# A Mamba-2 recurrence in chunks of 64 tokens instead of 128, two chunks side by side on the partitions

## The chip, the cores and the metric

The kernel runs on one core of a Trainium2 chip. Its engines are TensorE (PE; weight loads are listed apart as PEld), VectorE (DVE), ScalarE (ACT), GpSimd (POOL) and SyncE (SP), which issues nearly all DMAs. The metric is the device time of one launch in microseconds (us); lower is better. All arithmetic is in float32.

## The reference

The kernel computes one transformer-like layer on 8 sequences of 2048 tokens with 256 channels: a normalisation modulated by a condition, a Mamba-2 block, a gated residual, a second modulated normalisation, and 8 dense experts with a thresholded softmax gate. The change touches the recurrence of the Mamba-2 block, which the reference itself writes in chunks:

```python
CHUNK = 64                                   # NHEADS 8, HEADDIM 64, D_STATE 128
dA_cs = jnp.cumsum(dtc * A, axis=2)          # within a chunk
xt = xc * dtc[..., None]
diff = dA_cs[:, :, :, None, :] - dA_cs[:, :, None, :, :]
Lmat = jnp.where(causal, jnp.exp(diff), 0.0)
scores = jnp.einsum('bcihn,bcjhn->bcijh', Cc, Bc) * Lmat
y_diag = jnp.einsum('bcijh,bcjhp->bcihp', scores, xt)
decay_states = jnp.exp(dA_cs[:, :, -1:, :] - dA_cs)
states = jnp.einsum('bcjhn,bcjh,bcjhp->bchpn', Bc, decay_states, xt)
chunk_decay = jnp.exp(dA_cs[:, :, -1, :])
# scan over the chunks: s = chunk_decay * s + states; prev_states is s before each chunk
y_off = jnp.einsum('bcihn,bcih,bchpn->bcihp', Cc, jnp.exp(dA_cs), prev_states)
y = y_diag + y_off                           # + x * D, times silu(z), normalised, times W_out
```

The length of the chunk doesn't change the mathematical result: a longer chunk has a larger triangle of token pairs and fewer states.

## The kernel before, in words

The tokens are worked on in 32 blocks of T = 512 (4 for each of 8 sequences), each in NC = 4 chunks of P = 128 tokens. Each block passes through stages written as Python generators: `first_norm`, `project_xbc` (with `conv` and `steps_of_time`), `project_z`, `silu_xbc`, and for each chunk `spread`, `turn`, `within`, with `outputs` once for two chunks; then `output`, `gate_weights` and `experts`. A planner runs all generators on one simulated clock: a stage starts at its time in `STARTS` plus n * 70 us, each `yield` puts its next step later by so many us, `until` waits for a step of another stage, and `take` and `give` hand out the 8 PSUM banks (at most 4 for the use "m", two at once for the outputs). The order in which the steps come up is the order of the instructions on each engine; at run time each engine works through its own list in that order and waits on semaphores where data is missing. The plan's times are not enforced on the chip. So a changed `yield` changes the order alone.

The steps that the change touches:

- `steps_of_time` (L491): the step sizes dt of 8 heads for 4 chunks stand on 32 partitions a chunk. A scan (L526) forms the running sums `cs` of dt * A along the 128 tokens of a chunk, one DMA writes them to DRAM (L529), ACT forms the decays to the end of the chunk (L531), and PE turns dt, cs and the decays to token-major, `tok_major` (L535, L539).
- `spread` (L543): for each chunk a DMA spreads the sums of all heads over 128 partitions, `wide`, [128, 8 heads, 128 tokens].
- `turn` (L552): a transposing DMA brings x and B of the chunk token-major into `xtok`.
- `within` (L565): ACT forms for each head relu(cs_j - cs_i) on a 128x128 square, `w` (L575); PE forms the scores B.C (L585); ACT takes exponentials of `wide` (L586) and of `w` (L587); DVE scales x by dt (L590), masks the scores (L594) and multiplies them into `w` (L604); POOL scales x by the decays, `xdec` (L600), copies the decay of the whole chunk, `whole` (L608), and multiplies `wide` by C (L609). Then PE forms the state update B.xdec (L620), POOL decays the old state (L623), DVE adds (L634). Each state is [128 states, 512].
- `outputs` (L640): for two chunks, PE adds for each head x.w and state.wide into one PSUM bank a chunk (L652): 8 + 8 matmuls, 64 weight columns, 128 tokens each. DVE adds x * D (L664) and multiplies by silu(z) (L668); ACT squares (L675); POOL sums the squares to `sqs` (L677, L678).
- `output` (L685): 5.0 us of plan after the last outputs of a block, PE sums `sqs` over partitions (L693) and applies W_out (L706).

The other lines named in the prediction: L437 and L484 are the input projections, L366 the transposes of normalised tokens, L498, L733 and L812 small matmuls for dt, the gate and the expert biases, L741 and L772 transposes of the gate, L825 the experts' matmuls, and L782 their weighted sums on DVE.

Of the kernel before, what the change touches and what calls it, by code (L numbers as in the profile page):

```python
# [13 lines left out]
ALU = mybir.AluOpType  # L14
AX = mybir.AxisListType

P = 128
# [9 lines left out]
def kernel(  # L27
# [39 lines left out]
    NSB = L // T  # L67
    HALO = D_CONV - 1
    QD = P // NC
    assert NH <= QD and NH == 2 * MI and D_STATE == P and L % T == 0 and DI == NH * HEADDIM and DI <= 512 and CD == DI + 2 * P  # L70

    n_names = [0]
# [11 lines left out]

    ident = new(const, [P, P], "ident")
    make_identity(nc, ident)
    masks = new(const, [P, 2, P], "masks")
    ones, upper = masks[:, 0, :], masks[:, 1, :]
    nc.gpsimd.memset(ones, 1.0)
    make_upper_triangular(nc, upper, val=1.0, diag=True)  # L90
    neg_half = new(const, [P, NC], "neg_half")
    nc.gpsimd.memset(neg_half, -0.5)

# [397 lines left out]
    def steps_of_time(n):  # L491
# [31 lines left out]

        cs = new(sml, [P, P], "cs", bufs=1)
        nc.vector.tensor_scalar(u, dt, a_neg, None, ALU.mult)
        nc.vector.tensor_tensor_scan(cs, ones, u, 0.0, ALU.mult, ALU.add)  # L526
        yield 4.0
        d["cs_d"] = new(dram, [P, P], "cs_d")
        nc.sync.dma_start(out=d["cs_d"], in_=cs)  # L529

        nc.scalar.activation(e, cs, AF.Exp, bias=cs[:, P - 1 : P], scale=-1.0)  # L531
        yield 7.0
        t_ps = yield from take("m")
        for i, t in enumerate((dt, cs, e)):
# [8 lines left out]
    def spread(n, c):  # L543

        yield from until(info[n], "cs_d")
        wide = info[n]["wide", c] = new(chk, [P, NH, P], "wide", bufs=4)
        nc.sync.dma_start(
            out=wide, in_=info[n]["cs_d"][c * QD : c * QD + NH, :].partition_broadcast(P)
        )
        yield  # L550

# [13 lines left out]
    def within(n, c):  # L565


        d = info[n]
        yield from until(d, "tok", ("wide", c))
        xbc, tok_major, wide = d["xbc"], d["tok"], d["wide", c]  # L570
        tok = ts(c, P)
        bt, ct_ = xbc[:, MB, tok], xbc[:, MCC, tok]
        w = new(chk, [P, NH, P], "w", bufs=3)
        for h in range(NH):
            follow("act", nc.scalar.activation(  # L575
                w[:, h, :], wide[:, h, :], AF.Relu, bias=tok_major[:, 1, c, h : h + 1], scale=-1.0
            ))
            if h % 4 == 3:
                yield 1.6


        yield from until(d, ("xtok", c))

        s_ps = yield from take("m")
        nc.tensor.matmul(s_ps[:, :P], bt, ct_, start=True, stop=True)  # L585
        nc.scalar.activation(wide, wide, AF.Exp)  # L586
        nc.scalar.activation(w, w, AF.Exp, scale=-1.0)  # L587
        yield 1.2
        xdt, bm = d["xtok", c][:, :DI], d["xtok", c][:, DI:]
        follow("dve", nc.vector.tensor_tensor(  # L590
            by_head(xdt), by_head(xdt), per_head(tok_major[:, 0, c, :]), ALU.mult
        ))
        sm = new(chk, [P, P], "sm")
        nc.vector.tensor_mul(sm, s_ps[:, :P], upper)  # L594
        give(s_ps)
        last = s_of(n) == NSB - 1 and c == NC - 1
        yield 1.0
        if not last:
            xdec = new(chk, [P, DI], "xdec", bufs=1)
            nc.gpsimd.tensor_tensor(  # L600
                by_head(xdec), by_head(xdt), per_head(tok_major[:, 2, c, :]), ALU.mult
            )
        yield 0.6
        nc.vector.tensor_tensor(w, w, sm[:, None, :].to_broadcast([P, NH, P]), ALU.mult)  # L604
        yield 1.8

        whole, cw = new(chk, [P, NH], "whole", bufs=3), wide
        nc.gpsimd.tensor_copy(whole, wide[:, :, P - 1])  # L608
        nc.gpsimd.tensor_tensor(cw, wide, ct_[:, None, :].to_broadcast([P, NH, P]), ALU.mult)  # L609
        yield 2.0  # L610
        if c > 0:
            yield from until(d, ("state", c - 1))
        elif s_of(n) > 0:
            yield from until(info[n - 1], ("state", NC - 1))
        yield 5.5
        state = carry.get("state") if (s_of(n), c) != (0, 0) else None
        if not last:

            st_ps = yield from take("m")
            nc.tensor.matmul(st_ps[:, :DI], bm, xdec, start=True, stop=True)  # L620
            behind = new(blk, [P, DI], "state", bufs=4)
            if state is not None:
                nc.gpsimd.tensor_tensor(  # L623
                    by_head(behind), by_head(state), per_head(whole), ALU.mult
                )
            carry["state"] = behind
        d["state", c] = True
        d["parts", c] = [(xdt, w)] if state is None else [(xdt, w), (state, cw)]
        yield 1.5
        if not last:  # L630
            if state is None:
                nc.vector.tensor_copy(behind, st_ps[:, :DI])
            else:
                nc.vector.tensor_add(behind, st_ps[:, :DI], behind)  # L634
            give(st_ps)
        if c % 2:
            yield 1.5
            yield from outputs(n, c - 1)

    def outputs(n, first):  # L640
# [3 lines left out]


        pair = yield from take("y", 2)
        for j, y_ps in enumerate(pair):
            parts = d["parts", first + j]
            for i, (lhs, rhs) in enumerate(parts):
                for h in range(NH):  # L650
                    m, q = divmod(h, 2)
                    nc.tensor.matmul(  # L652
                        y_ps[ts(q, HEADDIM), ts(m, P)], lhs[:, ts(h, HEADDIM)], rhs[:, h, :],
                        start=(i == 0 and m == 0), stop=(i == len(parts) - 1),
                        skip_group_check=True,
                    )
        yield from until(d, *(("z_silu", m) for m in range(MI)))
        for j, y_ps in enumerate(pair):
            c = first + j
            tok = ts(c, P)  # L660
            yield 1.4
            y = y_ps.rearrange("p (m t) -> p m t", m=MI)
            for m in range(MI):
                nc.vector.scalar_tensor_tensor(  # L664
                    y[:, m, :], xbc[:, m, tok], d_ch[:, m : m + 1], y[:, m, :],
                    ALU.mult, ALU.add,
                )
            nc.vector.tensor_tensor(g[:, :, tok], y, g[:, :, tok], ALU.mult)  # L668
            give(y_ps)
            yield 1.8  # L670

            if c == 0:
                d["sqs"] = new(sml, [P, NC, P], "sqs", bufs=1)
            sq = new(chk, [P, MI, P], "sq", bufs=1)
            pace["act"] = nc.scalar.activation(sq, g[:, :, tok], AF.Square)  # L675
            yield 0.8
            nc.gpsimd.tensor_add(sq[:, 0:2, :], sq[:, 0:2, :], sq[:, 2:4, :])  # L677
            nc.gpsimd.tensor_add(d["sqs"][:, c, :], sq[:, 0, :], sq[:, 1, :])  # L678
            d["y", c] = True

    def s_of(n):
# [3 lines left out]
    def output(n):  # L685
# [1 line left out]
        d = info[n]  # L687
        yield from until(d, *(("y", c) for c in range(NC)))
        wo = gated[b][0]
        yield 5.0  # L690
        s_ps = yield from take("m")
        for c in range(NC):
            nc.tensor.transpose(s_ps[:, ts(c, P)], d["sqs"][:, c, :], ident)  # L693
# [199 lines left out]
```

## Time and profile before

| | |
|---|---|
| median of 3 runs | 2341.03 us (2340.72 to 2341.4) |
| span of the profiled execution | 2336.8 us |
| what lies around the span, against the median | 4.2 us |
| PE, PEld busy | 2250.2, 1253.1 us |
| DVE, ACT, POOL busy | 2010.7, 1505.5, 1192.7 us |
| data moved by DMA | 194.38 MB, 30.5% of 16 engines on SP's queue |

An instruction group is listed as line, engine, operation, what it writes from what it reads, shape and count, then its busy time and the mean of one in ns, then the idle time of its engine just before it and what ended that. `x16` in a timeline is sixteen instructions that follow each other, merged; the first column is the start, the second the time to the end of the last one. Ends of matmuls are modelled and overlap the next start, so times on PE are read from start to start. In a shape `128*64` the first number is the rows of the array that are used (the contraction), the second its columns (the width of the weights). Each matmul of the program appears as two MATMULs with a weight load each.

### The profile page before, as it was taken

How to read it: one execution, taken by the hardware profiler on the slowest of the kernel's cores; microseconds unless marked ns; L12 is line 12 of the kernel's file. 1: busy time of each engine (PE TensorE's matmuls, PEld its weight loads, DVE VectorE, ACT ScalarE, POOL GpSimd, SP SyncE). 2: the span in 40 equal slices, each digit the busy share in tenths (PEclk: the TensorE clock that was granted, in tenths of full speed). 3: DMA queues.
4: the chain of work that ended last, by engine and by line, in shares of the span. 5: the costliest groups of instructions: out<-in, count | busy, mean ns of one | idle time of the engine just before them, and what ended most of it. 6: DMA issues, size and time to landing. Idle time of an engine off the chain costs nothing.

```text
span 2336.8 us, 33023 instructions
## 1 busy us (share of the span) xinstructions
PE 2250.2 (96%) x10992; PEld 1253.1 (54%) x10992; DVE 2010.7 (86%) x4348; ACT 1505.5 (64%) x2871; POOL 1192.7 (51%) x1373
## 2 busy tenths in 40 slices
PE   6689999999999999999999999999999999999998
PEld 4344555555555555555555555555555555555564
DVE  5778898898888899888998889898898898888875
ACT  6775667676567675667665677665767666567620
POOL 2444446545456544555545545545556545456541
PEclk8899999999999999999999999999999999999999
DMA  6331324322323323323222323322323323323200
GB/s 202 90 87 47 92 78 91 87 76 77 88 77 101 87 69 79 92 77 101 82 73 83 89 82 95 83 73 81 101 77 91 83 72 81 92 77 91 83 24 18
DMA packets 255625, 194.38 MB, mean 83 GB/s; under 512 B 177592, under 2 KB 217568, under 8 KB 255456
## 3 DMA queue, kind: packets, MB, share of 16 engines
q1 hardware_dynamic: 255440, 192.27, 30.5%
q8 instruction: 88, 1.44, 0.3%
q14 instruction: 81, 0.66, 0.1%
q10 hardware_dynamic: 16, 0.01, 0.0%
HBM read 89.47 MB, written 60.82 MB: 64 GB/s over the span
## 4 chain that ended last, share of the span: by engine, by line
DVE 43%; ACT 22%; PE 22%; POOL 10%; issue 3%; DMA 1%; SPq 0%; POOLq 0%; ACTq 0%; DVEq 0%
DVE xbc L400 11%; PE bank L825 10%; DVE w L604 5%; DVE res L782 5%; ACT w L575 4%; PE bank L437 3%; DVE stats L343 3%; DVE bank L664 3%; ACT xbc L456 2%; POOL wide L609 2%; POOL rstd L339 2%; PE bank L652 2%; ACT wide L586 2%; ACT xn L356 2%; POOL sq L677 2%
## 5 line engine op out<-in xcount | busy, mean ns | idle before, releaser
L825 PE MATMUL bank<-we_sb,ht 128*128 128x512 f32 x2048 | 960.0, 597 | 5.9 <-DVE state L634 3.0
L825 PEld LDWEIGHTS bank<-we_sb,ht 128*128 128x128 f32 x2048 | 371.1, 191 | 361.5 <-issue 342.2
L782 DVE SCALAR_TENSOR_TENSOR res<-bank,wt,res 128x256 f32<-128x256 f32 x1024 | 485.8, 475 | 89.5 <-ACT res L818 47.3
L400 DVE SCALAR_TENSOR_TENSOR xbc<-bank,conv_w_sb,xbc 128x509 f32<-128x509 f32 (+2 forms) x576 | 423.6, 736 | 50.2 <-ACT halo L396 47.5
L437 PE MATMUL bank<-ht,w_in_sb 128*128 128x512 f32 x768 | 366.5, 601 | 2.0 <-ACT ht L368 2.0
L575 ACT ACTIVATE w<-wide,tok_major 128x128 f32<-128x128 f32 x1024 | 326.5, 395 | 0.0
L609 POOL TENSOR_TENSOR wide<-wide,xbc 128x1024 f32<-128x1024 f32 x128 | 303.2, 2369 | 10.2
L675 ACT ACTIVATE sq<-zs 128x512 f32<-128x512 f32 x128 | 80.3, 627 | 308.9 <-DVE zs L668 218.6
L356 ACT ACTIVATE xn<-xt,shift,rstd 128x256 f32<-128x256 f32 x256 | 134.4, 588 | 204.7 <-DVE shift L352 204.7
L706 PE MATMUL bank<-wo,zs 128*128 128x256 f32 x1024 | 243.2, 380 | 0.2 <-ACT res L818 0.2
L484 PE MATMUL bank<-ht,w_in_sb 128*128 128x512 f32 x512 | 243.1, 598 | 0.0
L600 POOL TENSOR_TENSOR xdec<-xtok,tok_major 128x512 f32<-128x512 f32 x120 | 149.8, 1249 | 177.2 <-issue 85.3
L706 PEld LDWEIGHTS bank<-wo,zs 128*128 128x128 f32 x1024 | 194.6, 190 | 80.8 <-issue 52.4
L604 DVE TENSOR_TENSOR w<-w,sm 128x1024 f32<-128x1024 f32 x128 | 218.1, 1704 | 21.7 <-ACT w L587 20.9
L392 ACT ACTIVATE xbc<-bank,conv_b_sb,conv_w_sb 128x512 f32<-128x512 f32 x192 | 147.3, 767 | 125.3 <-PE bank L437 125.0
L437 PEld LDWEIGHTS bank<-ht,w_in_sb 128*128 128x128 f32 x768 | 142.5, 194 | 143.7 <-issue 123.8
L790 POOL TENSOR_TENSOR res<-res,gates 128x256 f32<-128x256 f32 x128 | 101.5, 793 | 222.5 <-DVE res L782 213.5
L608 POOL COPY whole<-wide 128x8 f32<-128x8 f32 x128 | 28.1, 219 | 331.5 <-ACT wide L586 331.0
L664 DVE SCALAR_TENSOR_TENSOR bank<-xbc,d_ch,bank 128x128 f32<-128x128 f32 x512 | 171.0, 350 | 8.6 <-PE bank L652 1.8
L677 POOL TENSOR_TENSOR sq<-sq 128x256 f32<-128x256 f32 x128 | 111.7, 872 | 127.8 <-ACT sq L675 127.8
L484 PEld LDWEIGHTS bank<-ht,w_in_sb 128*128 128x128 f32 x512 | 94.7, 190 | 113.1 <-issue 112.1
L465 DVE COPY halves<-xbc 128x1024 uint16<-128x1024 uint16 x160 | 138.7, 884 | 15.7 <-ACT xbc L456 10.0
(128 smaller groups left out, 3431.0 us busy)
## 6 DMA issues: line engine op xcount, KB each, us to landing
wide<-cs_d SPq DMA_DIRECT2D x128, 512.0 KB
turned<-halves SPq DMA_DIRECT2D x160, 256.0 KB
out_dram<-xt SPq DMA_DIRECT2D x32, 512.0 KB
xt<-_attn_hidden_states_dram SPq DMA_DIRECT2D x31, 512.0 KB
cs_d<-cs SPq DMA_DIRECT2D x32, 64.0 KB
we_sb<-in_L_ffn_expert_w_dram SPq DMA_DIRECT2D x8, 256.0 KB
xtok<-turned SPq DMA_TRANSPOSE x128
ht<-in_L_wmod_dram SPq DMA_DIRECT2D x2, 512.0 KB
```

The source lines that it names most:

```text
L356: nc.scalar.activation(xn[:, c, :], src[:, c, :], AF.Identity, bias=shift[:, c : c + 1], scale=rstd[:, c : c + 1],)
L400: nc.vector.scalar_tensor_tensor(acc[:, ahead:], ps[:, : T - ahead], conv_w_sb[:, m, k : k + 1], acc[:, ahead:], ALU.mult, ALU.add,)
L437: nc.tensor.matmul(ps, w_in_sb[:, k, DI + m * P : DI + (m + 1) * P], ht[:, k, :], start=(k == 0), stop=(k == KD - 1),)
L484: nc.tensor.matmul(ps, w_in_sb[:, k, ts(m, P)], ht[:, k, :], start=(k == 0), stop=(k == KD - 1),)
L575: follow("act", nc.scalar.activation(w[:, h, :], wide[:, h, :], AF.Relu, bias=tok_major[:, 1, c, h : h + 1], scale=-1.0))
L604: nc.vector.tensor_tensor(w, w, sm[:, None, :].to_broadcast([P, NH, P]), ALU.mult)
L609: nc.gpsimd.tensor_tensor(cw, wide, ct_[:, None, :].to_broadcast([P, NH, P]), ALU.mult)
L664: nc.vector.scalar_tensor_tensor(y[:, m, :], xbc[:, m, tok], d_ch[:, m : m + 1], y[:, m, :], ALU.mult, ALU.add,)
L677: nc.gpsimd.tensor_add(sq[:, 0:2, :], sq[:, 0:2, :], sq[:, 2:4, :])
L706: nc.tensor.matmul(o_ps[:, :DM], d["zs"][:, m, ts(c, P)], wo[:, m, :], start=(m == 0), stop=(m == MI - 1),)
L782: pace["dve"] = nc.vector.scalar_tensor_tensor(res, ps[:, ts(q, DM)], wt[:, c, e + q : e + q + 1], res, ALU.mult, ALU.add)
L825: nc.tensor.matmul(ps, ht[:, k, ts(c, P)], we_sb[:, k, e : e + per, :].rearrange("p e o -> p (e o)"), start=(k == 0), stop=(k == KD - 1),)
```

## The change

Each 128-token chunk becomes two of 64 tokens, a = 0 and 1, that stand side by side on partitions 0 to 63 and 64 to 127. The running sums start anew at token 64 (`keep` has a zero there), and the decays are formed for each half. DRAM holds the sums as [chunk, half, head, 64 tokens], written by four DMAs; a second tile `own` gets, by two DMAs a chunk, the sums of its own half on each half of the partitions, and takes the place of `w`. The ramps, scores and inner products become 64x64 squares. The state is carried on every 64 tokens: two updates a chunk, each with 64 rows of the array, into two banks; two decays on POOL, two additions on DVE, the second half's after the first's. In the outputs a PSUM bank holds half a of both chunks, instead of one chunk, and DVE, ACT and POOL work on it in that order. Some planned delays change. The core of the diff:

```diff
-        nc.vector.tensor_tensor_scan(cs, ones, u, 0.0, ALU.mult, ALU.add)
+        nc.vector.tensor_tensor_scan(cs, keep, u, 0.0, ALU.mult, ALU.add)
         yield 4.0
-        d["cs_d"] = new(dram, [P, P], "cs_d")
-        nc.sync.dma_start(out=d["cs_d"], in_=cs)
-
-        nc.scalar.activation(e, cs, AF.Exp, bias=cs[:, P - 1 : P], scale=-1.0)
+        d["cs_d"] = new(dram, [NC, 2, NH, H], "cs_d")
+        for c in range(NC):
+            nc.sync.dma_start(
+                out=d["cs_d"][c].rearrange("a q t -> q a t"),
+                in_=cs[c * QD : c * QD + NH, :].rearrange("q (a t) -> q a t", a=2),
+            )
+        for a in range(2):
+            nc.scalar.activation(
+                e[:, ts(a, H)], cs[:, ts(a, H)], AF.Exp,
+                bias=cs[:, (a + 1) * H - 1 : (a + 1) * H], scale=-1.0,
+            )
...
+        own = info[n]["own", c] = new(chk, [P, NH, H], "own", bufs=4)
+        for a in range(2):
+            nc.sync.dma_start(
+                out=own[ts(a, H)].rearrange("p q t -> p (q t)"),
+                in_=cs_d[a].partition_broadcast(H),
+            )
...
-        w = new(chk, [P, NH, P], "w", bufs=3)
+        halves = [slice(c * P + a * H, c * P + (a + 1) * H) for a in range(2)]
         for h in range(NH):
             follow("act", nc.scalar.activation(
-                w[:, h, :], wide[:, h, :], AF.Relu, bias=tok_major[:, 1, c, h : h + 1], scale=-1.0
+                w[:, h, :], w[:, h, :], AF.Relu, bias=tok_major[:, 1, c, h : h + 1], scale=-1.0
             ))
             if h % 4 == 3:
-                yield 1.6
+                yield 1.2
...
-        nc.tensor.matmul(s_ps[:, :P], bt, ct_, start=True, stop=True)
+        for a, tok in enumerate(halves):
+            nc.tensor.matmul(
+                s_ps[ts(a, H), :H], xbc[:, MB, tok], xbc[:, MCC, tok],
+                start=True, stop=True, skip_group_check=True,
+            )
...
+        nc.vector.tensor_tensor(w, w, sm[:, None, :].to_broadcast([P, NH, H]), ALU.mult)
+        yield 1.8
+        whole = new(chk, [P, 2, NH], "whole", bufs=3)
+        nc.gpsimd.tensor_copy(whole, wide[:, :, :, H - 1])
+        for a, tok in enumerate(halves):
             nc.gpsimd.tensor_tensor(
+                wide[:, a], wide[:, a], xbc[:, MCC, None, tok].to_broadcast([P, NH, H]), ALU.mult
+            )
...
-        yield 5.5
+        yield 3.5
+        both = yield from take("m", 2)
+        for a, st_ps in enumerate(both):
+            if not (last and a):
+                nc.tensor.matmul(
+                    st_ps[:, :DI], bm[ts(a, H), :], xdec[ts(a, H), :], start=True, stop=True
                 )
+        states = d["before", c] = []
+        for a, st_ps in enumerate(both):
+            state = carry.get("state") if (s_of(n), c, a) != (0, 0, 0) else None
+            states.append(state)
+            if not (last and a):
+                behind = new(blk, [P, DI], "state", bufs=6)
+                if state is not None:
+                    nc.gpsimd.tensor_tensor(
+                        by_head(behind), by_head(state), per_head(whole[:, a, :]), ALU.mult
+                    )
+                carry["state"] = behind
...
+            yield 1.5
+            if not (last and a):
+                if state is None:
+                    nc.vector.tensor_copy(behind, st_ps[:, :DI])
+                else:
+                    nc.vector.tensor_add(behind, st_ps[:, :DI], behind)
             give(st_ps)
...
+        views = [y_ps.rearrange("p (m j t) -> p m j t", m=MI, j=2) for y_ps in pair]
+        for j in range(2):
+            xdt, w = d["inner", first + j]
+            for h in range(NH):
+                m, q = divmod(h, 2)
+                for a, y in enumerate(views):
+                    nc.tensor.matmul(
+                        y[ts(q, H), m, j, :], xdt[ts(a, H), ts(h, HEADDIM)], w[ts(a, H), h, :],
+                        start=(j == 0 and m == 0), stop=False, skip_group_check=True,
+                    )
+        for a, y in enumerate(views):
+            for j in range(2):
+                state, cw = d["before", first + j][a], d["wide", first + j][:, a]
...
                 for h in range(NH):
                     m, q = divmod(h, 2)
                     nc.tensor.matmul(
+                        y[ts(q, H), m, j, :], state[:, ts(h, HEADDIM)], cw[:, h, :],
+                        start=False, stop=True, skip_group_check=True,
                     )
...
-        yield 5.0
+        yield 9.0
         s_ps = yield from take("m")
```

## The prediction

> **What bounds the kernel now.** I read the page first, then the windows by stage, then PE's timeline over one block of 512 tokens (there are 32), then the groups by line and PE's waits. The page: PE is busy for 96% of the span at a granted clock of 0.9 or more outside the first tenth.
>
> ```profile
> PE 2250.2 (96%) x10992; PEld 1253.1 (54%) x10992; DVE 2010.7 (86%) x4348; ACT 1505.5 (64%) x2871; POOL 1192.7 (51%) x1373
> PE   6689999999999999999999999999999999999998
> PEclk8899999999999999999999999999999999999999
> ```
>
> The windows (us, then busy us of PE, PEld, DVE, ACT, POOL, clock, DMA share) show where PE's idle time lies:
>
> ```profile
> 200.00:700.00 500.00, 491.49 (x2410) 273.38 (x2410) 445.50 (x970) 329.08 (x629) 263.09 (x298) 1.00 0.32 83
> 700.00:1200.00 500.00, 494.54 (x2468) 276.65 (x2465) 444.51 (x971) 334.35 (x639) 264.06 (x299) 1.00 0.32 85
> ```
>
> In steady state PE idles 5 to 9 us in 500, DVE 55. A busy row alone proves little, since the ends of matmuls are modelled; the starts decide. PE's timeline:
>
> ```profile
> 1222.44 1.02 PE L620 MATMUL bank<-xdec,xtok 128*128 128x512 f32 x2
> 1223.39 1.09 PE L652 MATMUL bank<-w,xtok 128*64 128x128 f32 x16
> 1224.32 1.04 PE L652 MATMUL bank<-wide,state 128*64 128x128 f32 x16
> 1225.19 1.04 PE L652 MATMUL bank<-w,xtok 128*64 128x128 f32 x16
> 1226.06 1.04 PE L652 MATMUL bank<-wide,state 128*64 128x128 f32 x16
> 1227.04 1.98 PE L825 MATMUL bank<-we_sb,ht 128*128 128x512 f32 x4
> 1228.86 0.27 PE L772 MATMUL bank<-ident,wt 128*128 128x128 f32 x1
> 1228.97 0.39 PE L585 MATMUL bank<-xbc 128*128 128x128 f32 x2
> 1229.19 1.88 PE L825 MATMUL bank<-we_sb,ht 128*128 128x512 f32 x4
> 1231.00 1.13 PE L812 MATMUL bank<-eb_sb,wtt 64*128 64x256 f32 x8
> 1232.07 0.66 PE L366 MATMUL bank<-ident,xn 128*128 128x128 f32 x4
> ...
> 1239.45 1.89 PE L706 MATMUL bank<-wo,zs 128*128 128x256 f32 x8
> 1241.27 0.64 PE L498 MATMUL bank<-ht,w_dt 128*32 128x128 f32 x16
> 1241.84 1.12 PE L620 MATMUL bank<-xdec,xtok 128*128 128x512 f32 x2
> 1242.81 1.88 PE L825 MATMUL bank<-we_sb,ht 128*128 128x512 f32 x4
> 1244.52 0.38 PE L585 MATMUL bank<-xbc 128*128 128x128 f32 x2
> ```
>
> Three readings, from start to start of groups. (1) Price of a column: every matmul of the program is two MATMULs; four of 512 columns take 1.72 us, two of 128 take 0.22: per MATMUL 429 and 109 ns, so about 2.5 ns + 0.833 ns a column, and 56 ns for 64 columns. Groups follow each other without a gap: PE is the pace. (2) Tiles work side by side: sixteen of L652 take 0.87 us, 54.5 ns each, half of 109, since two heads use two 64-column tiles. L498 keeps four 32-column tiles busy (sixteen in about 0.44 us, 27 ns each), and L812 two row tiles (eight of 256 columns in about 0.86 us, where one after the other would take 1.73). (3) Leaving the full array costs: the group before a tiled one takes 1.81 or 1.82 us where it takes 1.72 elsewhere (L825 before L812; L706 before L498), the tiled one some 0.13 to 0.2 more than its columns, the first group of 512 columns after it 0.1 more (L825 after L652: 1.82; L620 after L498: 0.97 instead of 0.86). Together 0.35 us for an excursion: 0.10 us of draining and one weight load that is not hidden, at each change.
>
> The Trainium skill, "TensorEngine Tiling (Array Packing)", Key Properties, says that a change of tiling mode, not of tile, drains the TensorE; it speaks against this change, and the 0.35 us are this trace's price for it.
>
> **The change, part by part, on PE** (128 chunks of 128 tokens, 64 pairs).
> - *Inner products.* Before 2,048 MATMULs at 54.5 ns: 111.6 us. After 128 x 16 heads-and-halves x 2 = 4,096 of 64 columns. I take four 64x64 tiles at once (L498 shows four, L812 shows row tiles): 56/4 = 14 ns each, 57.3 us. Bounds: 14 ns below, 28 ns above (only the two column tiles at once, as L652), which is 57 us more.
> - *Products with the states.* Before 1,920 at 54.5: 104.6. After 248 halves (the first of each of 8 batches has no state) x 16 = 3,968 at 28 ns: 111.1.
> - *A change of mode between these two kinds* in each pair of chunks: 64 x (0.10 + 0.05) = +9.6.
> - *Scores.* Before 256 at 109 ns: 27.9; after 512 of 64 columns on two column tiles, 28 ns: 14.3, so -13.6. But L585 ran on the full array and is now an excursion, 128 x 0.35 = +44.8.
> - *State updates.* Before 240 at 429 ns: 103.0. After, two row tiles side by side hold the same 0.86 us for a chunk, 128 of them (the last chunk of a batch now has its first half): 109.8, +6.8. Each is an excursion too, with 128-column weight loads on both sides, 0.40 us as L812: +51.2.
>
> Sum: -47.8 + 9.6 + 31.2 + 58.0 = +51 us. Where a tiled group stands next to another tiled one, a change of mode (0.2 us) falls away. In the trace 31 scores stand before L733 (32-column tiles) and 54 L620 beside L652 or L498. The scores keep their place in the plan; the states are planned about 2 us earlier (5.5 becomes 3.5) and the outputs later relative to them (1.5+1.5 becomes 3 x 1.5), with a group of experts every 4.4 us, so I keep all 31 and a third of the 54: -10 us (bounds 0 and -17).
>
> The Trainium skill, "TensorE: Matmul & The Clock Gate", Part 1, puts a floor of about 25 ns on the distance between matmul starts. Single rows of L498 start 7 ns apart on different tiles (1241.269, 1241.275), so I don't apply it. By that rule the inner products would take 4,096 x 25 = 102 us, and the time would be some 45 us more than I say.
>
> **On the other engines.**
>
> ```profile
> L604 DVE TENSOR_TENSOR w<-w,sm 128x1024 f32<-128x1024 f32 x128 | 218.1, 1704 | 21.7 <-ACT w L587 20.9
> L609 POOL TENSOR_TENSOR wide<-wide,xbc 128x1024 f32<-128x1024 f32 x128 | 303.2, 2369 | 10.2
> L575 ACT ACTIVATE w<-wide,tok_major 128x128 f32<-128x128 f32 x1024 | 326.5, 395 | 0.0
> ```
>
> DVE: L604 halves (512 elements of SBUF take 849 ns in L590), -109 us; the smaller mask product -9; 128 more state adds at L634's 680 ns, +87: -31 us. ACT: the ramps L575 lose 64 elements, 8 x 52 ns a chunk, and the second Exp half of its 1,041: about -106, and +10 for two decays instead of one: -96 us. POOL: 120 more state products at L623's 1,282 ns, +154; L609 in two pieces of about 1,250 instead of 2,369, +17; 8 more xdec, +10: +181 us, 58% busy. None of the three gets over 86%, so none is credited or charged; the cover is PE, and if PE were not the pace DVE's 31 us would be the gain.
>
> DMA: `own` adds 128 x 256 KB to 192 MB, 5 points on a share of 30.5%. SP issues 256 + 96 more DMAs at 0.32 to 0.45 us (rows of L529, L547), 4.4 us a block. Behind them stand the copies of `halves` and the transposes into `xtok`; ACT waited 0.0 us for `wide` (L575), so I charge 0, and at most 10 us without that cover. `own` has four buffers, freed by the inner products, before those of `wide`, which come free later in the same group of outputs: no wait that `wide` hasn't already.
>
> New waits. POOL's second state product waits for DVE's first state add, and that for PE's state update. Today POOL runs 4 to 13 us ahead of PE at L623; this lead is lost once a chunk. Queued behind are `xdec`, the decays and the 1/sqrt of the next norms. DVE's second add waits in turn for POOL (1.05 to 1.3 us), with the next heads' work behind it. DVE's first add ends 2.0 to 4.9 us after L620 starts; the last quarter of the outputs, which needs it now, comes about 5 us after. So PE waits little: I take +6 us (none to 64, that is 0.5 us a chunk, as L741's waits are 1 us each).
>
> Waits that go:
>
> ```profile
> PE bank L693 <- POOL sqs L678: 24.1, 25, 5.9
> PE bank L741 <- ACT head L739: 8.3, 8, 1.1
> ```
>
> The stage of L693 is planned 9.0 instead of 5.0 after the outputs: of 24.1 us (half of them in the first two blocks) I take half back, -12 (bounds 0 and -24). Next late there is the chain through the sums of squares, with POOL busier. Start-up, three more small DMAs before the first chunk: +1.
>
> **Sum** against the profiled execution: 2336.8 + 51 - 10 + 6 - 12 + 1 = 2373 us of span. The median of the runs shown, 2341.03, is 4.2 above that span, so I predict 2377 us.
>
> **Rivals.**
> - *Only two tiles at once, or an issue limit, in the 64x64 products.* No row shows row and column tiles together, nor 128 such pairs in a row. +57: 2434 us. Against it: L498 and L812 each show their half.
> - *A new wait becomes the pace*: the chain PE, DVE, POOL, DVE of each chunk, or the second bank that a chunk now holds of eight. At 0.5 to 1 us a chunk, +58 to +122 over the forecast: 2435 to 2499. For it: DVE is 89% busy in steady state and stands in order. Against it: a chunk has 17.5 us, the chain about 5.
> - *Faster: the changes of mode cost much less than I charge.* The 105 us of excursions and mode changes decide. If a short tiled group drained little, say a third of my price, 70 us fall away: 2307 us. It turns at two thirds of the price (36 us less). Against it: L498, L812 and L652, of 0.4, 0.9 and 3.5 us, all show the same 0.35.
> - *All small terms the good way* (every neighbour kept, all 24 us of L693 gone, no new wait) gives 2341 + 51 - 17 - 24 + 1 = 2352: still slower. That the change doesn't do what it says is excluded by the diff.
>
> **How the numbers follow.** Forecast, between 2350 and 2405: 0.69. Two tiles at once: 0.11. A new wait: 0.11. Cheap changes of mode: 0.09, of which a part ends within the bound. The range goes from 2348 (all small terms good) to 2440 (either slower rival at its start). About 0.2%, 5 us, is what a measurement of this kernel can tell from no change. Slower 0.89, same 0.03, faster 0.08.
>
> **What would show it.** Right: PE again above 95%, span longer with PE's work; runs of 32 inner MATMULs in about 0.45 us; 0.1 us lost before and after each score and each update; L693's wait smaller; DVE and ACT less busy. Wrong: inner products at 28 ns each; idle time of PE before L620's successors or the outputs, released by DVE's state add; or scores and updates that follow their neighbours without the 0.1 us.

## The result and the profile after

The changed kernel takes 2560.18 us (2554.94 to 2562.95, 4 runs) against 2341.02: 1.094 times, 95% interval 1.0925 to 1.0956, so 219 us slower. The prediction had the sign right and 36 us instead of 219; the time lies 120 us above its range.

The page of the changed kernel, the lines that answer to those of before:

```profile
PE 2361.2 (92%) x15600; PEld 1217.2 (48%) x15600; DVE 1931.8 (76%) x4476; ACT 1470.5 (57%) x2947; POOL 1272.6 (50%) x1640
...
PE   7889999989999899999999989999999899998998
...
PEclk8989999999999999999999999999999999999999
```

The span is 2557.5 us. PE is no longer the pace: it is busy for 92%, and DVE, ACT and POOL are all less busy in share than before. The windows (us, then busy us of PE, PEld, DVE, ACT, POOL, clock, DMA share) say that this holds in steady state, where PE idled 5 to 9 us in 500:

```profile
200.00:700.00 500.00, 468.77 (x3126) 239.47 (x3124) 389.09 (x891) 297.78 (x598) 257.26 (x326) 0.98 0.32 87
700.00:1200.00 500.00, 461.57 (x2999) 236.23 (x3000) 374.44 (x884) 289.88 (x578) 246.20 (x316) 0.96 0.36 91
1200.00:1700.00 500.00, 469.54 (x3123) 242.05 (x3122) 385.45 (x904) 293.35 (x588) 252.95 (x325) 0.97 0.33 87
```

The clock column is new too: 0.96 to 0.98 where it was 1.00. From the records of PE and of the granted clock the 221 us between the two profiled spans can be split. PE's idle time rose from 87 to 196 us. Of its busy time I weighted each stretch with the clock granted in it: what was lost to a slow clock rose from 15 to 72 us, and the work that is left, at full clock, from 2235 to 2289 us:

| | before | after | difference |
|---|---|---|---|
| PE's work at full clock | 2235 | 2289 | +54 |
| lost to a slow clock while busy | 15 | 72 | +57 |
| PE idle | 87 | 196 | +110 |
| span | 2337 | 2557 | +221 |

So a quarter is work and three quarters are waits and what follows them. PE's work looks as forecast. PE's timeline, start and length, then group and count:

```profile
1215.94 1.89 PE L753 MATMUL bank<-wo,zs 128*128 128x256 f32 x8
1217.76 1.16 PE L684 MATMUL bank<-own,xtok 64*64 64x64 f32 x64
1218.85 2.08 PE L695 MATMUL bank<-wide,state 128*64 128x64 f32 x64
1220.77 0.29 PE L604 MATMUL bank<-xbc 128*64 128x64 f32 x4
1220.98 1.98 PE L441 MATMUL bank<-ht,w_in_sb 128*128 128x512 f32 x4
1222.81 1.88 PE L872 MATMUL bank<-we_sb,ht 128*128 128x512 f32 x4
```

64 inner MATMULs of 64x64 (L684) take 1.09 us with the change of mode behind them, 17 ns each: four tiles at once. 64 products with states (L695) take 1.92, 30 ns each. A score (L604) takes 0.21 to 0.27, the group before a tiled one 1.82, the group after it 1.83: the changes of mode at the price taken.

The waits of PE (how long in all, how often, the longest) show where the idle time lies:

```profile
PE bank L819 <- DVE wt L815: 73.4, 21, 5.5
PE bank L441 <- ACT ht L372: 22.9, 16, 2.0
PE bank L872 <- DVE zs L714: 14.2, 14, 1.9
PE bank L859 <- ACT wtt L822: 14.1, 11, 5.5
```

Before, the same transposition of the gate weights (L772 there, L819 here) never waited. Now it waits 3.5 us in two blocks of three, for the end of the gate's softmax on DVE. One such wait on PE's timeline:

```profile
1408.48 1.45 PE L872 MATMUL bank<-we_sb,ht 128*128 128x512 f32 x3
1415.47 0.45 PE L819 MATMUL bank<-ident,wt 128*128 128x128 f32 x1 [5.54 <-DVE wt L815]
1415.71 1.06 PE L370 MATMUL bank<-ident,xn 128*128 128x128 f32 x4
1416.59 2.04 PE L872 MATMUL bank<-we_sb,ht 128*128 128x512 f32 x2
1418.56 1.66 PE L859 MATMUL bank<-eb_sb,wtt 64*128 64x256 f32 x8
1420.15 1.12 PE L872 MATMUL bank<-we_sb,ht 128*128 128x512 f32 x2
```

and the same time in windows, from the groups before the wait to the groups after it (the last but two column is the clock):

```profile
1402.50:1409.90 7.40, 7.00 (x137) 4.49 (x136) 4.97 (x8) 4.92 (x6) 4.26 (x4) 1.00 0.27 91
1409.90:1415.40 5.50, 0.03 (x1) 0.00 (x0) 5.43 (x15) 0.00 (x0) 3.57 (x3) 0.77 0.64 201
1415.40:1420.20 4.80, 4.73 (x16) 2.56 (x16) 3.98 (x11) 3.11 (x6) 2.80 (x5) 0.56 0.74 215
1420.20:1424.00 3.80, 3.80 (x17) 1.89 (x16) 2.02 (x5) 3.80 (x12) 3.72 (x6) 1.00 1.12 219
```

PE stands still for 5.5 us, and then runs at a clock of 0.56 for nearly 5 us more: two MATMULs of 512 columns take 1.97 us instead of 0.86, L859 1.59 instead of the 1.07 of L812. By the record of the granted clock, the half clock began 2.9 us into the gap and lasted 6.8 us, of which 4.2 lie behind it: the 5.5 us of standing still cost about 2 us more. What DVE did in that time, from its timeline:

```profile
1400.77 0.18 DVE L800 TENSOR_REDUCE red<-lg 128x4 f32<-128x32 f32 x1
1403.56 1.30 DVE L469 COPY halves<-xbc 128x1024 uint16<-128x1024 uint16 x2 [2.62 <-ACT xbc L460]
1404.77 0.18 DVE L801 TENSOR_TENSOR lg<-lg,red 128x32 f32<-128x32 f32 x1
1404.88 0.68 DVE L664 TENSOR_TENSOR state<-bank,state 128x512 f32<-128x512 f32 x1
...
1406.71 0.69 DVE L664 TENSOR_TENSOR state<-bank,state 128x512 f32<-128x512 f32 x1 [0.76 <-POOL state L653]
1408.01 3.34 DVE L469 COPY halves<-xbc 128x1024 uint16<-128x1024 uint16 x2 [0.60 <-DMA turned<-halves]
1411.27 0.17 DVE L805 TENSOR_REDUCE red<-lg 128x4 f32<-128x32 f32 x1
...
1415.14 0.18 DVE L815 TENSOR_TENSOR wt<-wt,wsum 128x32 f32<-128x32 f32 x1
```

The gate's softmax (L800, L801, L805, L815) is cut apart by the copies of a later block into `halves` (L469), one of which waits 2.6 us for ACT, and by the state adds (L664), one of which waits 0.8 us for POOL. Before, all of those copies stood ahead of the softmax in the plan. Two suspects, then: the chain of states, and the order.

### The profile page after: what moved, and what is told of

It is laid out like the page before. It is cut to its first block, busy times and chain, and to the rows that moved or that the text cites. A ratio compares the mean times of both kernels' runs of the same rounds, so it can differ in the third digit from the quotient of the medians.

```text
span 2557.5 us, 43573 instructions
## 1 busy us (share of the span) xinstructions
PE 2361.2 (92%) x15600; PEld 1217.2 (48%) x15600; DVE 1931.8 (76%) x4476; ACT 1470.5 (57%) x2947; POOL 1272.6 (50%) x1640
## 5 line engine op out<-in xcount | busy, mean ns | idle before, releaser
L872 PE MATMUL bank<-we_sb,ht 128*128 128x512 f32 x2048 | 1001.7, 617 | 20.5 <-DVE zs L714 14.2
L441 PE MATMUL bank<-ht,w_in_sb 128*128 128x512 f32 x768 | 383.1, 621 | 22.9 <-ACT ht L372 22.9
L631 POOL TENSOR_TENSOR wide<-wide,xbc 128x512 f32<-128x512 f32 x256 | 341.3, 1351 | 33.4 <-ACT xbc L460 29.7
L621 POOL TENSOR_TENSOR xdec<-xtok,tok_major 128x512 f32<-128x512 f32 x128 | 140.4, 1097 | 428.5 <-PE bank L643 180.8
L653 POOL TENSOR_TENSOR state<-state,whole 128x512 f32<-128x512 f32 x240 | 260.4, 1085 | 163.4 <-DVE state L664 159.1
L593 ACT ACTIVATE own<-own,tok_major 128x64 f32<-128x64 f32 x1024 | 267.1, 344 | 0.0
L664 DVE TENSOR_TENSOR state<-bank,state 128x512 f32<-128x512 f32 x240 | 164.8, 687 | 106.2 <-POOL state L653 99.8
L488 PE MATMUL bank<-ht,w_in_sb 128*128 128x512 f32 x512 | 244.8, 602 | 0.2 <-DVE xbc L404 0.2
L721 POOL TENSOR_TENSOR sq<-sq 128x256 f32<-128x256 f32 x128 | 95.3, 745 | 260.7 <-ACT sq L719 226.1
L441 PEld LDWEIGHTS bank<-ht,w_in_sb 128*128 128x128 f32 x768 | 139.5, 196 | 164.9 <-issue 111.4
L469 DVE COPY halves<-xbc 128x1024 uint16<-128x1024 uint16 x160 | 155.1, 993 | 52.8 <-ACT xbc L460 39.4
L608 ACT ACTIVATE wide<-wide 128x1024 f32<-128x1024 f32 x128 | 134.4, 1054 | 79.3 <-DMA wide<-cs_d 78.8
```

Source lines behind the costliest of these rows:

```text
L441: nc.tensor.matmul(ps, w_in_sb[:, k, DI + m * P : DI + (m + 1) * P], ht[:, k, :], start=(k == 0), stop=(k == KD - 1),)
L469: SPLIT(halves, d["xbc"][:, m, :].bitcast(U16).rearrange("p (t n) -> p n t", n=2))
L488: nc.tensor.matmul(ps, w_in_sb[:, k, ts(m, P)], ht[:, k, :], start=(k == 0), stop=(k == KD - 1),)
L593: follow("act", nc.scalar.activation(w[:, h, :], w[:, h, :], AF.Relu, bias=tok_major[:, 1, c, h : h + 1], scale=-1.0))
L631: nc.gpsimd.tensor_tensor(wide[:, a], wide[:, a], xbc[:, MCC, None, tok].to_broadcast([P, NH, H]), ALU.mult)
L653: nc.gpsimd.tensor_tensor(by_head(behind), by_head(state), per_head(whole[:, a, :]), ALU.mult)
```

## The experiments

All times are against runs of the kernel before on the same chip, 2340 to 2342 us.

**Four first experiments.** e1 undoes the longer delay of the stage that sums the squares:

```diff
         wo = gated[b][0]
-        yield 9.0
+        yield 5.0
```

> The changed kernel with the stage of the sums of squares planned 5.0 us after the outputs again, instead of 9.0. Theory A (order: PE waits 73 us at L819 because the gate's softmax on DVE is planned right behind the copies into halves of the next block, which stand late): the gate's chain is planned 3 us earlier, but the copies still stand where they are, so the wait stays or grows: 2530 to 2600 us. Rival A' (it is this delay alone that makes the gate late): the 73 us at L819 and the slow clock behind them go: 2430 to 2470. Theory B (the chain of states between POOL and DVE holds DVE up): no change, 2550 to 2565.

Measured: 2666 us (1.1396, interval 1.1378 to 1.1414), 106 slower than the changed kernel. PE's waits:

```profile
PE bank L819 <- DVE wt L815: 102.7, 23, 7.3
PE bank L740 <- POOL sqs L722: 97.8, 28, 6.6
```

The time lies above theory A's range: the gate's wait grew, as A had it, and the sums of squares were late by 98 us on top. In this order the 9.0 was needed.

e2 puts other work of PE ahead of the wait:

```diff
         nc.vector.tensor_mul(w, w, over(wsum))
-        yield 8.0
+        yield 13.0
...
-        (silu_xbc, 47.5), (output, 144.0), (gate_weights, 172.0), (experts, 214.0),
+        (silu_xbc, 47.5), (output, 144.0), (gate_weights, 172.0), (experts, 219.0),
```

> The changed kernel with the transposition of the gate weights on PE (L819) planned 13.0 instead of 8.0 us after the softmax, and the experts at 219 instead of 214: PE gets other work ahead of that wait. Theory A (a wait at one place, by order): L819 waits under 15 us in all, PE's clock recovers by about half of its 57 us, 2440 to 2480 us. Theory B (DVE and POOL are late altogether because of the chain of states): the waits move to L441, L859 and the experts' banks, 2520 to 2565.

Measured: 2558 us (1.0937, interval 1.0918 to 1.0955), the same as the changed kernel. L819 waits hardly any more, but the waits moved:

```profile
PE bank L441 <- ACT ht L372: 84.8, 32, 6.1
PE bank L788 <- ACT head L786: 28.9, 14, 3.4
```

PE's idle time is 193 us, as it was 196. So taking away the wait at this one place brings nothing; the lateness shows elsewhere. Theory A falls in this form.

e3 breaks the chain between POOL and DVE:

```diff
-                        by_head(behind), by_head(state), per_head(whole[:, a, :]), ALU.mult
+                        by_head(behind), by_head(states[0] or state), per_head(whole[:, a, :]), ALU.mult
```

> The changed kernel, in which POOL's second product of a chunk takes the state before the chunk instead of the one that DVE has just added (the second half's state then lacks the first half's part; all instructions, sizes and transfers stay). POOL no longer waits for DVE, nor DVE for POOL, within a chunk. Theory B (this chain is the cause): POOL's 159 us and DVE's 100 us of waits at these lines fall under 30, L819's wait of PE under 20, time 2430 to 2480 us. Theory A (order): those waits of POOL and DVE go but PE's wait at L819 stays above 50, time 2520 to 2560.

Measured: 2572 us (1.099, interval 1.0972 to 1.1008), 12 slower than the changed kernel. PE still waits 60 us at L819 and idles 206. The waits of POOL and DVE for each other, in the changed kernel and then in e3:

```profile
POOL state L653 <- DVE state L664: 159.1, 129, 7.0
DVE state L664 <- POOL state L653: 99.8, 127, 5.9
```

```profile
POOL state L653 <- DVE state L664: 126.5, 52, 8.0
DVE state L664 <- POOL state L653: 10.8, 13, 4.5
```

DVE's wait went, but most of POOL's didn't, against both theories' expectation: the second product of a chunk no longer waits (108 us before), and the first, which takes the state that the chunk before has left, waits longer (some 130 us instead of 50). Cutting the chain inside the chunk wins nothing, which speaks against theory B, the rival that I had priced at up to 122 us. h1 below cuts it where POOL's waits go too.

e4 prices an excursion from the full array in the kernel before, with scores that are the same to the last column:

```diff
-        nc.tensor.matmul(s_ps[:, :P], bt, ct_, start=True, stop=True)
+        for a in range(2):
+            half = slice(c * P + a * (P // 2), c * P + (a + 1) * (P // 2))
+            nc.tensor.matmul(
+                s_ps[ts(a, P // 2), :P], xbc[:, MB, half], ct_,
+                start=True, stop=True, skip_group_check=True,
+            )
```

> The kernel before, with the 128x128 scores of a chunk formed by two matmuls of 64 weight columns on the two column tiles instead of one on the full array; nothing else. The same columns pass PE in the same time (0.22 us), so what is added is the price of leaving the full array, which I took as 0.35 us: 128 x 0.35 = 45 us less 31 x 0.2 beside L733 = +39: 2375 to 2390 us. If short excursions cost a third of it: 2350 to 2358. If they bring waits on other engines or a slow clock with them: above 2395.

Measured: 2349 us (1.0038, interval 1.0023 to 1.0053). PE's work rose by 33 us, 0.26 us a score, which is what 0.35 less the neighbours gives (39) within 6 us. The time rose by 8 alone, since PE's idle time fell from 87 to 64 us: a PE that is later by 33 us meets fewer late inputs; the instructions of all engines stand in the order of before, but for the added matmuls. So work added to PE doesn't pass whole into the time, not even with PE at 96%; I had passed it whole.

**The order.** After these, theory D: not the new instructions but the order in which all instructions stand is at fault. Two places in the change could have altered it. The state update takes two banks of eight. In the plan the input projections then wait 325 us for banks instead of 166, and all takers 693 instead of 221; the copies into `halves` come 6 us later against the block. f1 puts that shortage alone into the kernel before, with not one instruction of the program changed:

```diff
-            st_ps = yield from take("m")
+            st_ps, spare = yield from take("m", 2)
...
             give(st_ps)
+            yield 1.5
+            give(spare)
```

> The kernel before, in whose plan the state update takes two PSUM banks instead of one (the second is never written) and the second is given back 1.5 us later, as in the changed kernel. No instruction is added or changed: only the order shifts, since takers of banks wait longer in the plan (the input projections 329 us instead of 166 in all; the copies into halves are planned 6 us later, among the gate's softmax, as in the changed kernel). Theory D (the order that the bank shortage makes in the plan is what costs 160 us of PE idle time and slow clock): 2420 to 2500 us, with PE waits at L772 and L693. Rival E (the new instructions themselves, the excursions and the longer chains, cost it): 2335 to 2355 us.

Measured: 2449 us (1.0468, interval 1.0443 to 1.0492): 108 us from order alone, with PE's work within 7 us of before. PE waits at the places that the changed kernel showed:

```profile
PE bank L695 <- POOL sqs L680: 48.5, 20, 6.1
PE bank L774 <- DVE wt L770: 44.8, 16, 4.6
PE bank L743 <- ACT head L741: 20.3, 19, 1.7
```

(L695, L774 and L743 are the sums of squares, the gate weights and the gate's logits in this file.) The order also decides how often ACT loads an activation table, 1.28 us each: 254 times in f1, 211 before. The number of loads alone doesn't set the time: the changed kernel has 255, and i1 below, 152 us faster, 269.

f5 takes the shortage out of the changed kernel's plan again:

```diff
-    READ_TIME = 4.5
+    READ_TIME = 3.0
```

> The changed kernel, whose plan reckons that a bank is free 3.0 us after its last reader was planned, instead of 4.5 (a number of the plan alone). The waits for banks in the plan fall from 693 to 149 us, less than the 221 of the kernel before, and the copies into halves stand 6 us earlier again. Theory D: PE's idle time falls by 80 us or more and the clock recovers 40: 2400 to 2440 us, which leaves the work of 54 us. Rival E: 2530 to 2570 us.

Measured: 2488 us (1.063, interval 1.0609 to 1.0651), 72 us better, and the time lost to a slow clock back from 72 to 32 us. That is short of the 2400 to 2440 that D alone promised. f3 left the shortage and stretched the plan:

```diff
-    PERIOD, XBC_STEP, Z_STEP, OUT_STEP = 70.0, 6.0, 3.5, 4.4
+    PERIOD, XBC_STEP, Z_STEP, OUT_STEP = 75.0, 6.0, 3.5, 4.4
```

> The changed kernel planned with a period of 75.0 us a block instead of 70.0. PE's own work is now 71.5 us a block (2289 us in 32), more than the plan's period. If the plan's period being too short for the work is the cause (theory F), the order fits again: 2420 to 2480 us. Theory D: the bank waits in the plan hardly fall (544 instead of 693 us) and the copies into halves still stand among the gate's softmax: 2500 to 2600 us. Rival E: 2540 to 2570 us.

Measured: 2532 us (1.0812, interval 1.0793 to 1.0832), as D expected of it; a period shorter than the work (F) is not the main cause: the longer one wins 28 us of 219.

In f5 a wait stood out that the kernel before doesn't have at all; it is in the changed kernel too (ACT's waits, changed kernel, then f5):

```profile
ACT wide L608 <- DMA wide<-cs_d: 78.8, 40, 5.4
```

```profile
ACT wide L608 <- DMA wide<-cs_d: 136.6, 55, 6.8
```

ACT waits for the landing of `wide`. In the kernel before, the DMA of a chunk's `wide` was issued 32 to 55 us (median by place in the block) before its exponential; in the changed kernel 5 to 11. Nothing had become of the DMA: the exponential had moved. ACT's timeline in the changed kernel, where L608 is the exponential of `wide` and L593 the ramps:

```profile
1417.07 1.04 ACT L608 ACTIVATE wide<-wide 128x1024 f32<-128x1024 f32 x1
...
1420.03 0.33 ACT L593 ACTIVATE own<-own,tok_major 128x64 f32<-128x64 f32 x1
...
1421.21 1.07 ACT L593 ACTIVATE own<-own,tok_major 128x64 f32<-128x64 f32 x4
...
1422.84 0.82 ACT L593 ACTIVATE own<-own,tok_major 128x64 f32<-128x64 f32 x3
1423.56 1.05 ACT L608 ACTIVATE wide<-wide 128x1024 f32<-128x1024 f32 x1
```

The eight ramps between the two exponentials belong to the chunk before that of the first one. Counted over ACT's instructions in the trace, 118 of the 128 exponentials stand ahead of all ramps of their own chunk and of the chunk before; in the kernel before, each stood behind all ramps of its own chunk. The program builder places an instruction on its engine's list when it reckons its inputs ready, and the plan's order alone doesn't hold it, so the order of the steps is the order of the instructions only where a dependency keeps it; the kernel ties the ramps down (`follow`). Before, the ramps read `wide` and the exponential overwrote it, so it stood behind them. Now they read `own`, and that tie is gone. g1 puts one back:

```diff
-        nc.scalar.activation(wide, wide, AF.Exp)
+        tc.add_manual_dep(
+            nc.scalar.activation(wide, wide, AF.Exp).ins, relu.ins.name,
+            mybir.DependencyInfo(mybir.DependencyClass.NoSync, mybir.DependencyReason.DATA),
+            reason="in the order of emission",
+        )
```

where `relu` is the last ramp of the chunk.

> The changed kernel with one dependency more, for the order at build time alone: the exponential of wide (L608) comes after the last ramp of its chunk on ACT, as it did before, when the ramps read wide and the exponential overwrote it. Now the ramps read own, nothing ties it, and on ACT's list it stands a chunk ahead; ACT meets it 4 to 9 us after the issue of wide's DMA, which was 32 to 55 us before. Theory C (this exponential, run ahead of its chunk, blocks ACT on the landing of wide, 79 us, and lets POOL take the products with C early): ACT's wait for wide falls under 10 us, PE's idle time by 40 us or more, 2440 to 2520 us. Theory D alone (the bank order): ACT's wait goes but the time stays, 2530 to 2565 us.

Measured: 2509 us (1.0721, interval 1.0705 to 1.0737), 51 us better; ACT's wait for `wide` is gone from its list, and PE idles 155 us instead of 196. g2 has both:

> Both: the exponential of wide tied to its chunk, and the plan's 3.0 us for a bank. With 3.0 alone the time was 2488 us, with 137 us of ACT waiting for wide and 65 us of PE's idle time more than before. If C and D are the two causes and add up: PE's idle time under 110 us, 2400 to 2440 us, what is left over the kernel before being mostly PE's work (54 to 65 us). If C costs nothing: 2475 to 2500 us.

Measured: 2449 us (1.046, interval 1.0442 to 1.0477): 111 us off the changed kernel, nearly the sum of 51 and 72, and short of the range. And the control for the number 3.0:

> The kernel before with the plan's 3.0 us for a bank instead of 4.5: the control for these two. If 3.0 helps any order (PE idles 87 us, of which 24 at L693): 2300 to 2330 us, and then part of what the changed kernel won by it is not its own. If it only undoes the shortage that the change makes: 2335 to 2350 us. If the banks are then taken too early and PE waits for their readers: above 2360 us.

Measured: 2352 us (1.0052, interval 1.0037 to 1.0067): 11 us slower, so 3.0 is no gift to any order.

**What was left of g2.** Its PE does 2289 us of work, as the changed kernel, idles 121 and loses 41 to the clock. Once more the chain of states, on this better order, with the edit of e3:

> The kernel of g2 (exponential tied, 3.0 us for a bank), in which POOL's second product of a chunk takes the state before the chunk instead of the one DVE has just added (the second half's state lacks the first half's part; sizes, instructions and transfers stay). In g2 POOL waits 295 us for DVE at these products and DVE 82 us for POOL, and 60 us of PE's idle time and slow clock are left over the kernel before. If this chain holds them: 2395 to 2425 us. If it is covered, as it was in the order of the changed kernel: 2440 to 2460 us.

Measured: 2465 us (1.0533, interval 1.0517 to 1.0548), 16 slower, though POOL's waits for DVE at the state fell from 295 to 17 us. The chain is covered, here with the waits really gone, and theory B falls. Then the delay of 9.0, first in the kernel before, where the prediction had let it win 12 us:

```diff
         wo = gated[b][0]
-        yield 5.0
+        yield 9.0
```

> The kernel before with the stage of the sums of squares planned 9.0 us after the outputs instead of 5.0, nothing else: the step of the prediction that was to give 12 us back. As predicted: L693's 24 us fall under 10 and nothing else is late: 2322 to 2336 us. If the order is what counts, the later gate meets the next block's copies and experts and PE waits at L741 or L772 instead: 2345 to 2400 us.

Measured: 2362 us (1.0092, interval 1.0076 to 1.0109). L693's wait fell as predicted, and the later gate waited instead (PE's waits):

```profile
PE bank L741 <- ACT head L739: 23.3, 16, 1.7
PE bank L620 <- POOL xdec L600: 11.0, 7, 5.6
PE bank L733 <- ACT ht L368: 7.7, 6, 1.5
PE bank L772 <- DVE wt L768: 6.8, 6, 2.2
PE bank L693 <- POOL sqs L678: 6.5, 3, 4.7
```

21 us lost, where I had booked 12 won. i1 takes it back in g2 (edit of e1):

> The kernel of g2 with the stage of the sums of squares planned 5.0 us after the outputs again. If the late gate (54 us of PE's waits at L793 and L785 in g2) is what is left: 2420 to 2438 us. If the sums of squares are too late for it, as they were in the changed kernel's own order (98 us of waits there in e1): 2455 to 2540 us.

Measured: 2408 us (1.0296, interval 1.0278 to 1.0313), below the favourable range, and the opposite of e1's sign. Its page and a window:

```profile
PE 2311.5 (96%) x15600; PEld 1193.1 (50%) x15600; DVE 1960.5 (81%) x4476; ACT 1481.9 (62%) x2961; POOL 1299.3 (54%) x1640
```

```profile
700.00:1200.00 500.00, 491.43 (x3387) 252.02 (x3386) 417.38 (x962) 320.96 (x637) 281.52 (x350) 1.00 0.36 97
```

PE is at 96% again and the clock at 1.00. Against the profiled kernel before: work +58, idle +8, clock +4 us, of 69 us of span. With three changes that concern order alone, what is left is PE's work.

i2 and i3 take the scores of g2 and of i1 back to the full array:

```diff
-        for a, tok in enumerate(halves):
-            nc.tensor.matmul(
-                s_ps[ts(a, H), :H], xbc[:, MB, tok], xbc[:, MCC, tok],
-                start=True, stop=True, skip_group_check=True,
-            )
+        nc.tensor.matmul(
+            s_ps[:, :P], xbc[:, MB, ts(c, P)], xbc[:, MCC, ts(c, P)], start=True, stop=True
+        )
...
-        nc.vector.tensor_mul(sm, s_ps[:, :H], upper[:, :H])
+        for a in range(2):
+            nc.vector.tensor_mul(sm[ts(a, H)], s_ps[ts(a, H), ts(a, H)], upper[ts(a, H), :H])
```

> The kernel of g2 with the scores of a chunk as one matmul of 128 tokens on the full array, of which the two 64x64 squares on the diagonal are used, with one mask product for each (2 x some 0.2 us of DVE instead of 1). PE's work falls by the price of 128 excursions, 32 us by e4. If PE's work passes through to the time: 2408 to 2425 us. If the waits take its place, as in e4 where the work rose by 33 us and the time by 8: 2435 to 2450 us.

> Both of these on g2. If the two add up as the favourable cases say: 2385 to 2410 us, the best form of this change, and still slower than before by the state updates' and the outputs' changes of mode. If the delay of 5.0 hurts: above 2440 us.

Measured: i2 2451 us (1.0476, interval 1.046 to 1.0492), i3 2442 us (1.0433, interval 1.0418 to 1.0449). PE's work fell by 19 and 20 us, and waits took its place: idle time rose by 20 us in i2 over g2 and by 44 in i3 over i1. The order is hardly the reason in i2: on PE, ACT, POOL and DVE some 99% of the instructions that it shares with g2 stand in the same order. Whether the second mask product on DVE is, or PE coming earlier to inputs that are late, wasn't separated.

## Why the prediction was wrong, point by point

- *PE's work: right, but for 13 us.* The five steps, +51 us, less 10 for neighbours make +41; the trace says +54. The changes of mode held at the price taken, and the rival of two tiles at once is out. By the trace, 46 tiled groups follow another tiled one, besides the two parts of the outputs, 27 of them scores right behind the products with states: some 9 us at the price taken, near the 10 booked. From start to start inside their groups the inner products stand 14.6 ns apart instead of 14 and the products with states 29.2 instead of 28, which is 7 of the 13 us; the rest is open.
- *"So PE waits little: I take +6 us (none to 64)", and "-12" for L693: the steps that failed.* In their place stand 110 us more of idle time. Both were worked out as if every other instruction kept its place, and many did not. L693's own wait fell even further than booked, from 24.1 to 6.7 us (L740), but the delay of 9.0 that brought it costs the kernel before 21 us (h2), because others then wait.
- *The slow clock: not in the sum at all.* 57 us, behind 110 us more of idle time. The record of the granted clock shows either full speed or half, and half for 3.41 us or a multiple of it (but at the run's end). In the changed kernel it fell to half 31 times, before 7 times; in the 3.41 us ahead of a fall PE had been idle for 1.7 us or more, in the wait shown above for 2.9. The Trainium skill, "TensorE: Matmul & The Clock Gate", HAM oscillation, has as its rule no idle gaps of PE above about 3.4 us; in this trace shorter ones were enough. A new wait of 2 or 3 us on PE should thus have been priced with a slow clock behind it.
- *"or the second bank that a chunk now holds of eight": the half of a rival that was right.* 108 us in the kernel before (f1), 72 in the changed one (f5), where I had named 58 to 122. I gave it 0.11 together with the chain, which wins nothing when it is cut (e3, h1), and looked for the price in a shortage on the chip, not in the plan.
- *"no wait that `wide` hasn't already": true of the buffers, and beside the point.* What changed for `wide` was a write-after-read on ACT that had kept its exponential in place: 51 us (g1).
- *The other engines.* ACT was to lose 96 us and lost 35: its table loads rose from 211 to 255, at 1.28 us each, which took 56 back. POOL was to gain 181 and gained 80: its products with the states took 1,085 ns on average (L653), not 1,282, which is 37 us of the difference although there were 128 more of them, not 120, and others of its instructions got shorter too (`xdec` from 1,249 to 1,097 ns). DVE lost 79 instead of 31. None of the three was the pace, as assumed.

What the runs show together: the change itself costs PE's work, 54 to 58 us; some 150 us of the 219 are order, since i1, with the same instructions, sizes and transfers (and 14 table loads more), takes 2408 us. Which displaced instruction makes PE late isn't shown. The place of the copies into `halves` doesn't settle it: on DVE 69 of the 160 stand inside a gate's softmax in the changed kernel, 1 in the kernel before, 85 in f1 and 1 in f5, but 2 in e2, which is no faster than the changed kernel, and 56 in h2, which loses only 21 us. The three causes found don't simply add: the delay of 9.0 costs 41 us behind the other two and wins 106 without them. Why the sums of squares were so late in e1 alone wasn't tried. No form of the change came under the kernel before.

## What to carry to other kernels

When a kernel's order is made by a plan, a change to a buffer's count or to what an instruction reads is a change to the order of everything: read the new lists before costing the new instructions, and look for ties that were only a side effect of overwriting a tile. A test that alters the plan and no instruction, as f1, prices this in one run. Where PE is the pace, price its waits with the clock behind them (57 us for 110 here), and expect work added or removed on it to trade with its idle time (33 us of work gave 8 in e4, and 20 us less gave nothing in i2).

## What the runs showed of the hardware that was not expected

- Four 64x64 tiles of float32 run at once with one weight load for each 64 columns: 17 ns a MATMUL over 64 of them, the change of mode included. Inside a group four of them, on four tiles, start 6 or 7 ns apart and the next four some 58 ns behind the first. The Trainium skill, "TensorE: Matmul & The Clock Gate", Part 1, has about 25 ns as the least distance of two starts; this trace is below it where the MATMULs go to different tiles.
- POOL's products of a state with its decays took 1,085 ns on average in the changed kernel and 1,282 before, with DVE at 76% instead of 86%. DVE's load alone isn't the reason: with DVE at 81% in both, they took 1,060 ns in f5 and 1,213 in f1. The reason is open.
- The clock of PE fell to half behind as little as 1.7 us of idle time in the 3.41 us before (changed kernel, 31 falls).
